# Two cross-attention layers on one core: half products in another order, two of them moved ahead of layer 0's last batch, layer 1's first scores moved ahead of the last query product, and a last pass in two halves

## The chip, the cores and the metric

The kernel runs on one core of a Trainium2 chip, in float32. The metric is the device time of one execution in microseconds (us); lower is better. A difference is judged between medians of runs made on the same chip.

## The reference, cut to what matters

There are 8 batches. `x` is (8, 100, 1024), the context `c` is (8, 1444, 512). Layer 0 is ordinary cross attention with an output projection, layer 1 takes its softmax over the 100 queries (axis 1) instead of over the keys and ends in a layer norm:

```python
# layer 0, per batch
Q = x @ Wq + bq;  K = c @ Wk + bk;  V = c @ Wv + bv
w = softmax(Q @ K.T / 32, axis=keys)
x = x + (w @ V) @ Wo + bo
# layer 1, per batch
q = x @ Wq + bq;  k = c @ Wk + bk;  v = c @ Wv + bv
w = softmax(q @ k.T / 32, axis=queries)
x = w @ v + x
out = (x - mean) * rsqrt(var + 1e-6) * gamma + beta
```

## The kernel before, in words

**Products of weights first.** The kernel never forms K or V. It multiplies Wq by Wk transposed once for each layer (`weight_products` "qk0", "qk1") and Wv by Wo ("vo0"). For a batch it then needs three things: `gT`, the queries times the first product (`queries`, 4 batches of 100 queries side by side in a half, so 400 columns); the scores, `gT` times the context's features (`scores`); and `A`, the weights times the context's rows (`weighted_rows`). `A` is projected at the end: for layer 0 by `project0` for all 8 batches at once, for layer 1 by `project1_halves` (batches 0 to 4), `project1` (5 and 6) and `project_last` (7).

**Seven products for eight.** `queries`, `project0` (twice, j = 0 and 1, tiles `o0_0` and `o0_1`) and `project1_halves` are block products of a 2 by 2 matrix of weight blocks A11, A12, A21, A22 and a 2 by 2 matrix of data blocks B11, B21, B12, B22. `seven_products` computes them with seven half products instead of eight, on sums of blocks: S[0] to S[3] of the A's (`left_sums`), T_[0] to T_[3] of the B's (`right_sums`), made by VectorE (DVE) in between. A half product accumulates in a pair of PSUM banks: X, Z and Y from a pool of 6 banks, W from a pool of 2. X is used three times in a row without being cleared: A11·B11, then S[1]·T_[1] on top, then S[2]·T_[2] on top. After each of these its content is copied or added into one of the four results. `put` is the first write of a result (ScalarE, ACT, in `queries`; an addition into `xT` on DVE elsewhere), `add` a later addition on DVE.

**Order.** TensorE's (PE's) order is the order of the program text (`tc.manual_schedule(engines={PE})`); the other engines' instructions are put in order by the tile framework's scheduler, each engine then running its own list strictly in order, with semaphores in between. In the program text: weight products, `queries(0)`, scores of batches 0 and 1, then for each batch b `alternated`: 48 steps, each one piece of A of batch b and one piece of the scores of batch b+2 (44 pieces). For b = 5 in each layer it takes two pieces of scores a step (`doubled`). Then `project0`, `queries(1)`, the key biases of layer 1 (`key_biases`, tile `c1`), scores of batches 0 and 1 of layer 1, and the 8 steps of `alternated` for layer 1 with the projections.

**Softmax and transposes.** Scores lie with the queries on the partitions and the weights must lie with the keys on them. Layer 0 does its softmax first (`softmax0`) and then transposes: on DVE in 16 instructions (`transposed`, L562), except that for batches 0 and 7 the first 4 of 12 key blocks are transposed on PE (`first_transposed`, tile `pT`, L578) and DVE does the other 8. Layer 1 transposes first and then takes the softmax by groups of 4 key blocks (`softmax_rows`); batch 0's 12 blocks are all transposed on PE, in three groups between the scores of batch 1 (`first_rows`).

**GpSimd (POOL)** makes layer 1's weight sums (`weight_sums`, tiles `part` and `wsum`), the block sums of the last weight (`wv_s`, eight additions) in the buffer that `qk1` leaves when the last query product has read it, and a part of each batch's end. **The end** of a batch is `normalise`: `rstd` on POOL, then for batch 7 three quarters of the row on DVE and one quarter on ACT and POOL, each followed by its store (SP's and ACT's queue).

Of the kernel before, what the change touches and what calls it, by code (L numbers as in the profile page):

```python
# [25 lines left out]
AF = mybir.ActivationFunctionType  # L26
ALU = mybir.AluOpType
# [26 lines left out]
def two_layer_cross_attention(ctx: ExitStack, tc: tile.TileContext, a: dict, out: bass.AP):  # L54
# [11 lines left out]
    def bank(name):  # L66
        return psum.tile([P, 512], F32, tag="ps", name=name)

    def bank2(name):
        return psum2.tile([P, 512], F32, tag="ps2", name=name)  # L70
# [48 lines left out]
    for t in prob:  # L119
        nc.gpsimd.memset(t[T // QD * QD :, :], 0.0)  # L120
        nc.gpsimd.memset(t[:, S:], 0.0)

# [39 lines left out]

    def seven_products(name, A, Bs, S, T_, nb, width, put, add, left=None, right=None):

        left, right = left or (lambda n: None), right or (lambda n: None)
        A11, A12, A21, A22 = A
        B11, B21, B12, B22 = Bs  # L170
        X, Z, Y = ([bank(f"{name}_{n}{j}") for j in range(2)] for n in "xzy")
        W = [bank2(f"{name}_w{j}") for j in range(2)]
        half_product(X, A11, B11, True, nb, width)
        put(0, 0, X)
        left(0)
        right(0)
        half_product(Z, A12, B21, True, nb, width)
        left(1)
        right(1)
        add(0, 0, Z)  # L180
        half_product(Y, S[0], T_[0], True, nb, width)
        put(1, 1, Y)
        left(2)
        right(2)
        half_product(X, S[1], T_[1], False, nb, width)
        put(0, 1, X)
        left(3)
        right(3)
        half_product(X, S[2], T_[2], False, nb, width)
        add(1, 1, X)  # L190
        put(1, 0, X)
        half_product(W, A22, T_[3], True, nb, width)
        add(1, 0, W)
        half_product(Y, S[3], B22, False, nb, width)
        add(0, 1, Y)


    def weight_products(name, left, right, l_width, r_width, scaled):
# [175 lines left out]
    def queries(layer, w, u):  # L374

        H = EC // 2

        def half(g):
            return xT[:, :, g * GT : (g + 1) * GT]

        cols = [slice(j * 256, j * 256 + 256) for j in range(2)]
        A11, A12, A21, A22 = ([w[:, k * H + i, c] for i in range(H)] for c in cols for k in range(2))
        Bs = [[half(g)[:, k * H + i, :] for i in range(H)] for g in range(2) for k in range(2)]
        S1, S2 = (chunks(row(f"g{layer}_s{n}").rearrange("p (c l) -> p c l", c=H), H) for n in (1, 2))
        T1, T2 = (chunks(wide(f"g{layer}_t{n}"), H) for n in (1, 2))
        T3 = chunks(work.tile([P, LC, GT], F32, tag="gT", name=f"g{layer}_t3", bufs=3), H)
        dst = [work.tile([P, LC, GT], F32, tag="gT", name=f"g{layer}T_{g}", bufs=3) for g in range(2)]
        A, S, T_ = (A11, A12, A21, A22), (S1, S2, A21, A12), (T1, T2, T3, T2)

        def put(r, g, banks):  # L390
            for j in range(2):
                c = 2 * r + j
                nc.scalar.activation(dst[g][:, c, :], banks[j][:, :GT], AF.Identity, bias=u[:, c : c + 1])  # L393

        def add(r, g, banks):
            for j in range(2):
                to = dst[g][:, 2 * r + j, :]
                nc.vector.tensor_tensor(to, to, banks[j][:, :GT], ALU.add)

        seven_products(  # L400
            f"g{layer}",
            A,
            Bs,
            S,
            T_,
            2,
            GT,
            put,
            add,
            lambda n: left_sums(A, S, (n,)),  # L410
            lambda n: right_sums(Bs, T_, (n,)),
        )
        return dst


    wqk0, (acc_c, acc_u) = weight_products(
# [11 lines left out]
    block_sums("u0", acc_u, sums_u)  # L428
    sums_c = quarter_sums("c0")
    block_sums("wqbk0", acc_c, sums_c[:, :EC, :])  # L430
    gT = [queries(0, wqk0, totals("u0", sums_u, LC)), None]
    block_sums("bvo", acc_o, sums_c[:, EC:, :])
    got = totals("wqbk0", sums_c, 2 * EC)
    wqbk0 = got[:, :EC]
# [104 lines left out]
    def softmax0(s, parts):  # L539

        b, p = s["b"], s["p"]
        maxima = small.tile([T, len(parts)], F32, tag="maxima", name=f"maxima_{b}")
        for n, part in enumerate(parts):
            nc.vector.tensor_reduce(maxima[:, n : n + 1], p[:, part], AX.X, ALU.max)  # L544
        negmax = small.tile([T, 1], F32, tag="negmax", name=f"negmax_{b}")
        nc.vector.tensor_reduce(negmax, maxima, AX.X, ALU.max, negate=True)
        total = small.tile([T, 1], F32, tag="total", name=f"total_{b}")
        nc.scalar.activation(p, p, AF.Exp, bias=negmax, accum_out=total)
        rtotal = small.tile([T, 1], F32, tag="rtotal", name=f"rtotal_{b}")
        nc.vector.reciprocal(rtotal, total)  # L550
        nc.scalar.activation(p, p, AF.Copy, scale=rtotal)
        transposed(s, PT if b in (0, B - 1) else 0)

    def transposed(s, m0):

# [45 lines left out]
    def project0(AS, A0):  # L601

        Bs = [[A0[g][:, 2 * k + i, :] for i in range(2)] for g in range(2) for k in range(2)]
        t12, t4 = (work.tile([P, LC, GT], F32, tag="gT", name=f"o0_t{n}", bufs=3) for n in (12, 4))
        T_ = ([t12[:, i, :] for i in range(2)], [t12[:, 2 + i, :] for i in range(2)], Bs[2], chunks(t4, 2))
        for j, (A, S) in enumerate(AS):

            def add(r, g, banks):
                e = 4 * j + 2 * r
                add_to_queries([e, e + 1], g * GT, GT, banks)  # L610

            right = None if j else (lambda n: right_sums(Bs, T_, (n,)))
            seven_products(f"o0_{j}", A, Bs, S, T_, 2, GT, add, add, right=right)


    def softmax1(s, parts):

        if s["b"]:
            transposed(s, 0)
            for m in range(0, MC, GM):  # L620
                softmax_rows(s, m)
            weight_sums(s)

    def softmax_rows(s, m0):
        b, w, r = s["b"], s["w"], shown(m0)
# [48 lines left out]
    def project1_halves(A, S, At):  # L674

        n = G1 * T // 2
        Bs = [[At[:, 2 * k + i, g * n : (g + 1) * n] for i in range(2)] for g in range(2) for k in range(2)]
        t1 = work.tile([P, LC, GT], F32, tag="gT", name="o1_t1", bufs=3).rearrange("p c t -> p (c t)")
        T_ = ([t1[:, i * n : (i + 1) * n] for i in range(2)], Bs[0], Bs[2], Bs[1])

        def add(r, g, banks):
            add_to_queries([4 * r + i for i in range(4)], g * n, n, banks)

        seven_products("o1", A, Bs, S, T_, 4, n, add, add, right=lambda k: right_sums(Bs, T_, (k,)))

    def project1(b0, n, A, between):

# [39 lines left out]
    def normalise(s):  # L727
# [7 lines left out]
        if b < B - 1:  # L735
# [1 line left out]
            nc.gpsimd.tensor_tensor(z, z, beta[:T], ALU.add)  # L737
            nc.gpsimd.dma_start(out=out[b], in_=z)
            return
        w, rest = slice(0, 3 * E // 4), slice(3 * E // 4, E)  # L740
        nc.scalar.activation(z[:, rest], z[:, rest], AF.Copy, scale=rstd)
        nc.gpsimd.tensor_tensor(z[:, rest], z[:, rest], beta[:T, rest], ALU.add)
        nc.vector.scalar_tensor_tensor(z[:, w], z[:, w], rstd, beta[:T, w], ALU.mult, ALU.add)
        nc.sync.dma_start(out=out[b][:, w], in_=z[:, w])
        nc.scalar.dma_start(out=out[b][:, rest], in_=z[:, rest])

    def finish(s):

# [18 lines left out]
    batches = [{"b": b} for b in range(B)]  # L767
    A0 = [wide(f"A0T_{g}") for g in range(2)]

    def run(*parts):  # L770

        parts = list(parts)
        while parts:
            parts = [g for g in parts if next(g, parts) is not parts]

    def loaded(*loads):

        got = [[] for _ in loads]
# [2 lines left out]
                to.append(next(load))  # L781
        return got

    def first_scores(layer, softmax, between):

        for b in range(2):
            steps = scores(batches[b], layer, *loaded(load_features(b)), softmax, alone=True)
            for n in range(LC * NB):
                next(steps)
                if b == 1 and n in between:  # L790
                    between[n]()

    def alternated(b, layer, softmax, dst, doubled=False):

# [11 lines left out]
            yield  # L806

    key_bias = [c0, None]
    first_scores(0, softmax0, {LC * NB - 3: lambda: first_transposed(batches[0], 0)})
    for b in range(B):  # L810
        steps = alternated(b, 0, softmax0, A0[b // G][:, :, b % G * T : (b % G + 1) * T], b + 3 == B)
        for n, _ in enumerate(steps):
            if (b, n) == (B - 2, MC * LC - PT - 1):
                first_transposed(batches[B - 1], 0)
        if b == 1:
            AS = value_sums(wvo)
    project0(AS, A0)

    gT[1] = queries(1, wqk1, u1)
    kb1 = [key_bias_sums(f"kb1_{g}", g * GT, (g + 1) * GT, wqbk1) for g in range(B // G)]  # L820
    key_bias[1] = key_biases("c1", kb1, bqbk1)
    vectors = [unit(f"vectors_{j}") for j in range(2)]
    gamma, beta = (t[:, :E] for t in vectors)
# [5 lines left out]
    wv1 = weights.tile([P, LC, E], F32, tag="w", name="wv1")  # L829
    nc.gpsimd.dma_start(out=wv1, in_=a["L1_xattn_Wv"].rearrange("(c p) e -> p c e", p=P))  # L830

    def first_rows(m0):
        first_transposed(batches[0], m0)
        softmax_rows(batches[0], m0)
        if m0 == MC - GM:
            weight_sums(batches[0])

    first_scores(1, softmax1, {5 + m0 // 2: lambda m0=m0: first_rows(m0) for m0 in range(0, MC, GM)})
    A1 = {}

    finished = {(B - 2, 0): 0, (B - 2, 14): 1, (B - 2, 28): 2, (B - 1, 6): G1, (B - 1, 22): G1 + 1}
# [49 lines left out]
```

## Time and profile before

| | us |
|---|---|
| median of 3 runs | 648.43 (647.94 to 648.45) |
| profiled execution, its own time | 647.25 |
| its span, first to last instruction | 645.5 |
| PE busy in the span | 634.1 |
| DVE busy | 438.8 |
| ACT busy | 134.6 |
| POOL busy | 102.4 |
| granted PE clock | 0.997 |

The profiled execution took 1.75 us more than its span. Times in the text are from the span's start. A line of the timeline gives start, length, engine, source line, operation, output<-input, shapes, count, and in square brackets how long the engine had been idle and what released it. PE is the matmul row, PEld the weight loads, which run ahead of it. The trace has two records for each float32 matmul, so a half product of 8 matmuls is "x16". The chain of waits shows, in order of time, the work that ended last at each moment.

### The profile page before, as it was taken

Reading aid. Unit: us, or ns where it says so; the run is one execution under the profiler, and the core shown is the slowest. Engines: PE = TensorE matmul, PEld = TensorE weight load, DVE = VectorE, ACT = ScalarE, POOL = GpSimd, SP = SyncE. Lnnn points to the kernel's source line nnn. Section 1 sums busy time; section 2 is a strip of 40 time slices with the busy share of each in tenths; the row PEclk is TensorE's granted clock in tenths of the full one; section 3 lists DMA queues with packets and bytes.
Section 4 is the critical chain, followed back from the end, with each engine's and each line's share of the span. In section 5 each row is a group of like instructions: output and inputs, shape, how many; then the busy total and the mean of one; then the engine's idle time right before and its main releaser. Section 6 shows DMA issues by size and latency. Waiting matters only on the chain.

```text
span 645.5 us, 9860 instructions
## 1 busy us (share of the span) xinstructions
PE 634.1 (98%) x3936; PEld 519.3 (80%) x3936; DVE 438.8 (68%) x831; ACT 134.6 (21%) x342; POOL 102.4 (16%) x122
## 2 busy tenths in 40 slices
PE   9999999999999999999999999999999999999994
PEld 8886445568885999999998555557999999989992
DVE  5999959569624775566753887214767655896994
ACT  1010010100204223322320000205433244330221
POOL 5000000019100000000010000052210222211773
PEclk9999999999999999999999999999999999999998
DMA  8937027000099789988997003037889889930122
GB/s 296 384 103 301 0 91 295 0 1 0 2 322 348 270 307 318 315 301 318 316 331 261 1 1 131 0 104 275 298 285 329 315 295 324 318 124 1 52 79 74
DMA packets 47961, 127.28 MB, mean 197 GB/s; under 512 B 3944, under 2 KB 6604, under 8 KB 47916
## 3 DMA queue, kind: packets, MB, share of 16 engines
q1 hardware_dynamic: 45454, 119.73, 53.5%
q0 software_dynamic: 2064, 6.56, 3.1%
q8 instruction: 31, 0.51, 0.3%
q10 hardware_dynamic: 398, 0.36, 0.2%
q14 instruction: 14, 0.11, 0.1%
HBM read 123.36 MB, written 3.28 MB: 196 GB/s over the span
## 4 chain that ended last, share of the span: by engine, by line
PE 84%; issue 5%; POOL 5%; DVE 3%; ACT 2%; POOLq 0%; ACTq 0%; DVEq 0%
PE s L515 23%; PE A L486 20%; PE qk_x L135 7%; PE g_x L135 5%; PE qk_y L135 4%; PE g_y L135 3%; PE vo_x L135 3%; DVE w L562 3%; PE o_x L135 3%; POOL z L737 2%; PE qk_w L135 2%; PE qk_z L135 2%; PE vo_y L135 2%; PE o_y L135 2%; PE g_w L135 2%
## 5 line engine op out<-in xcount | busy, mean ns | idle before, releaser
L486 PE MATMUL A<-w,c 120*128 120x100 f32 (+1 forms) x1536 | 242.8, 266 | 0.0
L486 PEld LDWEIGHTS A<-w,c 120*128 120x128 f32 (+1 forms) x1536 | 213.6, 190 | 0.5
L562 DVE STREAM_TRANSPOSE w<-prob 32x384 f32<-32x384 f32 (+1 forms) x240 | 132.4, 552 | 38.1 <-POOL wsum L654 16.6
L515 PE MATMUL s<-cT,g1T 128*100 128x131 f32 (+2 forms) x592 | 119.4, 296 | 0.0
L515 PE MATMUL s<-cT,g0T 128*100 128x131 f32 (+2 forms) x592 | 119.0, 296 | 0.0
L515 PEld LDWEIGHTS s<-cT,g0T 128*100 128x100 f32 x592 | 77.6, 167 | 8.3
L515 PEld LDWEIGHTS s<-cT,g1T 128*100 128x100 f32 x592 | 77.5, 167 | 7.7
L527 ACT ACTIVATE prob<-s,c 100x393 f32<-100x393 f32 (+2 forms) x64 | 35.1, 559 | 123.3 <-PE s L515 122.9
L632 ACT ACTIVATE w<-w,negmax 120x100 f32<-120x100 f32 (+1 forms) x96 | 34.8, 364 | 65.5 <-DVE negmax L630 65.5
L442 POOL TENSOR_SCALAR xT<-xT,L_xattn_bo 128x800 f32<-128x800 f32 x8 | 20.7, 2607 | 133.0 <-PE qk_x L135 133.0
L544 DVE TENSOR_REDUCE maxima<-prob 100x1 f32<-100x394 f32 (+3 forms) x32 | 16.3, 528 | 24.1 <-ACT prob L527 23.8
L135 PE MATMUL qk_x<-qk 128*128 128x256 f32 x128 | 29.5, 390 | 0.0
L649 POOL TENSOR_TENSOR part<-w 120x500 f32<-120x500 f32 x8 | 10.0, 1246 | 114.8 <-PE s L515 47.3
L135 PEld LDWEIGHTS qk_x<-qk 128*128 128x128 f32 x128 | 24.7, 197 | 4.0 <-ACT qk L253 0.4
L826 POOL DMA_DIRECT2D vectors<-in_L_xattn_gamma x1 | 0.6, 602 | 161.9 <-DVE rtotal L550 161.9
L630 DVE TENSOR_REDUCE negmax<-w 120x4 f32<-120x400 f32 (+1 forms) x24 | 12.7, 555 | 13.2 <-ACT w L579 13.1
L277 DVE SCALAR_TENSOR_TENSOR qk_L_xattn_bk<-qk,L_xattn_bk,qk_L_xattn_bk 128x1024 f32<-128x1024 f32 x14 | 17.9, 1280 | 3.4 <-DMA qk<-in_L_xattn_WqT 3.3
L632 ACT ACTIVATION_READ_ACCUMULATOR w<-w,negmax 120x1 f32 (+1 forms) x96 | 17.9, 186 | 0.0
L737 POOL TENSOR_TENSOR z<-z,vectors 100x1024 f32<-100x1024 f32 x7 | 16.5, 2356 | 8.3 <-ACT z L736 8.3
L393 ACT ACTIVATE g1T<-g_x,k 128x400 f32<-128x400 f32 x6 | 3.6, 594 | 63.4 <-PE g_x L135 58.1
L585 DVE TENSOR_TENSOR xT<-xT,o_x 128x400 f32<-128x400 f32 (+1 forms) x24 | 13.6, 601 | 4.5 <-PE o_x L135 4.2
L736 ACT ACTIVATE z<-z,rstd 100x1024 f32<-100x1024 f32 x7 | 8.0, 1148 | 41.2 <-POOL rstd L733 41.1
(218 smaller groups left out, 881.3 us busy)
## 6 DMA issues: line engine op xcount, KB each, us to landing
cT<-in_ctxT SPq DMA_DIRECT2D x64, 722.0 KB, 6.6
c<-in_ctx SPq DMA_DIRECT2D x48, 768.0 KB, 6.2
c<-in_ctx SPq DMA_DIRECT2D x16, 512.0 KB, 6.6
vo<-in_L_xattn_Wo SPq DMA_DIRECT2D x8, 512.0 KB, 6.8
qk<-in_L_xattn_WqT SPq DMA_DIRECT2D x8, 512.0 KB
qk<-in_L_xattn_WqT SPq DMA_DIRECT2D x15, 256.0 KB, 5.4
qk<-in_L_xattn_WkT SPq DMA_DIRECT2D x15, 256.0 KB, 6.2
c<-in_ctx SPq DMA_DIRECT2D x16, 224.0 KB, 5.9
```

The source lines that it names most:

```text
L135: nc.tensor.matmul(banks[n // per][:, n % per * width : (n % per + 1) * width], lhs[i][:, n * P : (n + 1) * P], rhs[i], start=(fresh and i ...
L277: nc.vector.scalar_tensor_tensor(acc, src, cols[v][:, h : h + 1], acc, ALU.mult, ALU.add)
L442: nc.gpsimd.tensor_scalar(xT[:, e, :], xT[:, e, :], out_bias[:, e : e + 1], None, ALU.add)
L486: nc.tensor.matmul(ps[:, k * T : (k + 1) * T], c[m // CQ][:r, m % CQ, k * P : (k + 1) * P], w[:r, m, :], start=(m == 0 and k == 0), stop=( ...
L515: nc.tensor.matmul(banks[n // per][:T, cuts[n] - o : cuts[n + 1] - o], q[:, k, t0 : t0 + T], cT[k][:, cuts[n] : cuts[n + 1]], start=(k == ...
L527: nc.scalar.activation(p[:, part], ps[:T, : part.stop - part.start], AF.Identity, bias=key_bias[layer][:T, b : b + 1], scale=SCALE,)
L544: nc.vector.tensor_reduce(maxima[:, n : n + 1], p[:, part], AX.X, ALU.max)
L562: nc.vector.transpose(blocks(w, r, m0 * T + q * QD, T, MC - m0), blocks(p, q, m0 * MR + r * QD, MR, MC - m0),)
L585: nc.vector.tensor_tensor(to, to, ps[:, : n * width].rearrange("p (n t) -> p n t", n=n), ALU.add)
L630: nc.vector.tensor_reduce(negmax[:r], w[:r, grp, :], AX.X, ALU.max, negate=True)
L632: nc.scalar.activation(w[:r, m0 + m, :], w[:r, m0 + m, :], AF.Exp, bias=negmax[:r, m : m + 1], accum_out=total[:r, m : m + 1])
L737: nc.gpsimd.tensor_tensor(z, z, beta[:T], ALU.add)
```

## The change

Six things, with their place in the code.

1. `seven_products` is a generator with a `yield` after each product. W (A22·T_[3]) moves from sixth to fifth place, between the second and the third use of X, and `right(3)` moves ahead of the second one. In `queries` T_[3] is written into T1's buffer instead of T2's.
2. `project0` yields its two generators. Before layer 0's batch 7 the first two products of `o0_0` (A11·B11 and A12·B21, which need batches 0 to 3 alone) are run; after it the first product of `o0_1`, then the rest.
3. Layer 0's b = 5 is no longer doubled, and batch 7's weights are all transposed on DVE (16 instructions over 12 blocks instead of 8; the 4 PE transposes and their ACT copy go).
4. In layer 1 six of the seven query products are issued, then the key biases' sum, then batch 0's scores, then the seventh product (S[3]·B22 into Y), then batch 1's scores.
5. In layer 1 batch 0's weights are transposed on DVE (16 instructions) and go through the same `softmax1` as the others; the 12 PE transposes and their three ACT copies go.
6. `normalise` for batch 7: two halves on DVE, the first stored by SP's queue, the second by ACT's; the ACT and POOL quarter goes.

On the engines: PE has the same matmuls less 16 transposes; SP's list is the same but for one store's size; POOL's list loses one instruction.

```diff
     def seven_products(...):
...
+        X = pair("x")
+        product(X, A11, B11, True)
         put(0, 0, X)
+        yield
+        Z = pair("z")
+        product(Z, A12, B21, True)
+        yield
         left(0)
         right(0)
-        half_product(Z, A12, B21, True, nb, width)
         left(1)
         right(1)
         add(0, 0, Z)
-        half_product(Y, S[0], T_[0], True, nb, width)
+        Y = pair("y")
+        product(Y, S[0], T_[0], True)
         put(1, 1, Y)
+        yield
+        right(3)
+        product(X, S[1], T_[1], False)
+        put(0, 1, X)
+        yield
         left(2)
         right(2)
-        half_product(X, S[1], T_[1], False, nb, width)
-        put(0, 1, X)
+        W = pair("w", bank2)
+        product(W, A22, T_[3], True)
+        yield
         left(3)
-        right(3)
-        half_product(X, S[2], T_[2], False, nb, width)
+        product(X, S[2], T_[2], False)
         add(1, 1, X)
         put(1, 0, X)
-        half_product(W, A22, T_[3], True, nb, width)
         add(1, 0, W)
-        half_product(Y, S[3], B22, False, nb, width)
+        yield
+        product(Y, S[3], B22, False)
         add(0, 1, Y)
+        yield
...
-        A, S, T_ = (A11, A12, A21, A22), (S1, S2, A21, A12), (T1, T2, T3, T2)
+        A, S, T_ = (A11, A12, A21, A22), (S1, S2, A21, A12), (T1, T2, T3, T1)
...
-        transposed(s, PT if b in (0, B - 1) else 0)
+        transposed(s, 0 if b else PT)
...
     for b in range(B):
-        steps = alternated(b, 0, softmax0, ..., b + 3 == B)
-        for n, _ in enumerate(steps):
-            if (b, n) == (B - 2, MC * LC - PT - 1):
-                first_transposed(batches[B - 1], 0)
+        if b == B - 1:
+            o0 = list(project0(AS, A0))
+            next(o0[0])
+            next(o0[0])
+        run(alternated(b, 0, softmax0, ...))
...
-    project0(AS, A0)
-    gT[1] = queries(1, wqk1, u1)
+    next(o0[1])
+    for steps in o0:
+        run(steps)
+    gT[1], steps = queries(1, wqk1, u1)
+    for n in range(6):
+        next(steps)
...
-    first_scores(1, softmax1, {5 + m0 // 2: lambda m0=m0: first_rows(m0) for m0 in range(0, MC, GM)})
+    run(first_scores(0, 1, softmax1))
+    run(steps)
+    run(first_scores(1, 1, softmax1))
...
-        w, rest = slice(0, 3 * E // 4), slice(3 * E // 4, E)
-        nc.scalar.activation(z[:, rest], z[:, rest], AF.Copy, scale=rstd)
-        nc.gpsimd.tensor_tensor(z[:, rest], z[:, rest], beta[:T, rest], ALU.add)
-        nc.vector.scalar_tensor_tensor(z[:, w], z[:, w], rstd, beta[:T, w], ALU.mult, ALU.add)
-        nc.sync.dma_start(out=out[b][:, w], in_=z[:, w])
-        nc.scalar.dma_start(out=out[b][:, rest], in_=z[:, rest])
+        for half, queue in ((slice(0, E // 2), nc.sync), (slice(E // 2, E), nc.scalar)):
+            nc.vector.scalar_tensor_tensor(z[:, half], z[:, half], rstd, beta[:T, half], ALU.mult, ALU.add)
+            queue.dma_start(out=out[b][:, half], in_=z[:, half])
```

## The prediction

> **What bounds the kernel now.** First the table of busy time, then the chain of waits, then the timeline where the chain shows a gap.
>
> ```profile
> PE 634.1 (98%) x3936; PEld 519.3 (80%) x3936; DVE 438.8 (68%) x831; ACT 134.6 (21%) x342; POOL 102.4 (16%) x122
> ```
>
> PE is busy 634.1 of 645.5 us, so time can only come from three places: PE work that goes, holes that the busy figure hides (a matmul's end is modelled), and the tail after PE's last product. The chain around the half products shows hidden holes:
>
> ```profile
> 404.21 5.37 PE g_x L135 x16
> 409.58 0.01 issue
> 409.59 5.64 PE g_x L135 x16
> 415.24 5.37 PE g_w L135 x16
> ```
>
> Equal products take 5.37 us, the third use of X 5.64. The weight loads, ACT and, for layer 1's projection, PE say why:
>
> ```profile
> 409.59 0.30 PEld L135 LDWEIGHTS g_x<-g_t,qk 128*128 128x128 f32 x2 [0.65 <-ACT g1T L393]
> 415.28 1.27 ACT L393 ACTIVATE g1T<-g_x,k 128x400 f32<-128x400 f32 x2 [5.06 <-DVE g1T L398]
> 575.56 3.54 PE L135 MATMUL o_x<-A1T,wv_s 128*128 128x250 f32 x16
> 580.35 3.64 PE L135 MATMUL o_x<-A1T,wv_s 128*128 128x250 f32 x16 [1.26 <-DVE xT L585]
> ```
>
> PE waits for ACT to copy X out before it adds the next product onto X; in `project1_halves` it waits for DVE. The second line also shows that ACT's copy of a bank starts only when DVE's addition from that bank is done. PE's other avoidable work is its transposes and the doubled batch:
>
> ```profile
> 308.25 0.45 PE s L515 x4
> ...
> 322.36 15.61 PE A L486 x140
> 337.97 0.34 PE pT L578 x4
> ...
> 439.56 0.35 PE pT L578 x4
> ...
> 441.13 0.34 PE pT L578 x4
> ...
> 442.69 0.35 PE pT L578 x4
> ```
>
> [...] a piece of A alone (128 weight columns, 100 moving) takes 15.61/70 = 0.223 us, and alternated with a score piece (100 weight columns, 131 moving) the pair takes 0.4275 (446.52 to 446.95). [...] batch 4's L734 took 3.34 us at 609.32 beside POOL's addition that ended at 611.58, against 1.28 elsewhere, but 16 DVE transposes kept 0.591 each beside POOL's sums at 448.
>
> **The change part by part.**
>
> *W between X and X.* The hole goes where a product of W's length hides the copy: 5.64 − 5.37 = 0.27 in each `queries` (124.64 and 409.59), 5.63 − 2·2.69 = 0.25 in each half of `project0` (358.01, 377.08), and in `project1_halves` 580.35 − 575.56 − 3.38 = 1.41 plus 0.10 of a slow restart. Sum 2.55 us. What W now needs earlier is T_[3]. In `queries` its first write waits until Y has read T1: done about 0.6 us after Y's end, W starts 5.37 after it. In `project1_halves` its second block comes after the Y additions, at 579.71 before; W would start at 578.94 and reach that block at 580.63, so 0.9 us is left. In layer 0's `queries` the next weight product's first DVE sums take T1's buffer and so wait for W (130.0 instead of 119.3), with X's additions of this product queued behind them; they are for a product that starts at 155, and X's banks are next needed at 141 to 148. I take nothing.
>
> *PE transposes.* Batch 7: 0.35. Layer 1's batch 0: 1.04. Sum 1.39, and four ACT copies off the path. DVE gets 16 transposes of 12 blocks instead of 8 (9.46 against 7.32 us), and 16 new ones (9.46).
>
> *Batch 5 not doubled.* Before, 22 steps of one A and two score pieces took 14.11 (308.25 to 322.36) and the 22 A pieces that follow 22·0.223 = 4.91: 19.02. Taken per step, 0.651·22 + 4.91 = 19.23. Now 44·0.4275 = 18.81. Gain 0.2 to 0.4; I take 0.4.
>
> *Does batch 7 still come in time?* Its scores now end with b = 5's 44th step, at 308.03 + 18.81 = 326.84, and A of batch 5 at 327.7. Batch 6, never doubled, shows the chain that follows: A of batch 4 ended at 308.03 and DVE's last of 16 transposes at 312.15 + 9.46 = 321.61, 13.6 later. So batch 7's weights are there at 341.3. PE reaches A of batch 7 at 327.7 + 48·0.223 = 338.4 without the two products of `o0_0`: 2.9 us too early. They add 2·2.69 = 5.38, to 343.8: covered by 2.5 us. DVE then adds them to `xT` beside A of batch 7. They are the same products, so PE gains and loses nothing by the move. After batch 7, Y of `o0_0` needs T_[0], two sums behind the copy of A: copy and sums took from 349.97 to 351.64 before, 1.7 us; the first product of `o0_1` covers 2.69.
>
> *Layer 1's start.* With E the end of the sixth query product, batch 0's scores need banks. The key biases' sum and the first score piece take free ones; the second and third take X's, held until ACT's copy, which waits for DVE's addition. Read from 415.07 to 416.55, ACT is done at E + 0.8 and E + 1.5; the pieces are due at E + 0.75 and E + 1.36. Lost: 0.1 to 0.35, I take 0.2. The fourth waits for DVE's reading of the key-bias bank, at about E + 1.6, and is due later. Call S the scores' end (16 pieces of 0.611). The seventh product (5.37) and batch 1's scores (9.77) follow: A of batch 0 starts at S + 15.1. By the rows of batch 1 before, DVE starts to transpose at S + 0.65, ends at S + 10.1, and the first four blocks' softmax is done 3.4 later; one addition of the seventh product, 0.5, is in DVE's list between. Ready at S + 14.0, 1.1 us early. But POOL's eight sums now fall here:
>
> ```profile
> 426.07 2.49 POOL L146 TENSOR_TENSOR wv_s<-wv 128x512 f32<-128x512 f32 x2 [39.61 <-PE g_y L135]
> ```
>
> They start when the seventh product ends, S + 5.4, and last 9.8 us, to S + 15.2. DVE's first multiplication (L636, two SBUF inputs) can wait for one of them, 1.25: lost 0 to 0.3, I take 0.1. POOL's weight sums of batch 0 start at S + 16.5; their transpose on PE comes a batch later.
>
> *The end.* DVE's 768 columns end at 640.51 and ACT's store is issued at 641.12, behind POOL's quarter, which waited for DVE. Two halves of 0.69 from 639.49 let the last store be issued at about 640.9: 0.2 gained, against 200 KB instead of 100 KB on that queue. No row shows how long a lone store of each size takes; POOL's 400 KB stores landed in 3.2 us. Between −0.3 and +0.3; I take +0.1. DVE, ACT and POOL before it follow PE's products and move with them.
>
> **Sum.** 2.55 + 1.39 + 0.4 − 0.2 − 0.1 + 0.1 = 4.1 us of 647.25, giving 643.1 for such an execution. That one ran 1.2 under the median of 648.43; against the median, **644.3**. Everything gained lies on PE before its last product, so nothing is taken off twice.
>
> **The rivals.**
>
> *Covers partly fail.* DVE runs in order, and each start (A of batch 7, `project0`'s Y, A of layer 1's batch 0) has a margin of only 1 to 2.5 us. If one or two are late by 1 to 2 us more than the rows say, the gain is 1.5 to 3.2: about 646. For it: the margins. Against: the chains were read off equal batches, and DVE is 33.35 of 38 us busy in 350 to 388, where the change takes four additions away.
>
> *DVE behind POOL at layer 1's start: slower.* If POOL's eight sums keep DVE out for their whole length, DVE's chain of batch 0 stretches by up to 9.9 us. 1.1 is margin, so PE stands up to 8.8 us at A of batch 0: 648.43 − 4.1 + 8.8 = 653.1. It decides from a delay of 1.1 + 4.1 = 5.2 us. For it: the 3.34 us above. Against: transposes have run beside POOL undisturbed[...].
>
> *Holes move.* If W's product only moves the wait (T_[3] late in each of the five places by as much as the hole was), 2.55 goes and the rest, 1.6 less small losses, stays: 646.9. Against: DVE had T_[3]'s sums done in 2 to 3 us in all three kinds of place. That PE's transposes do not go, or that the order is not what the text says, is excluded by the instruction lists.
>
> **How the numbers follow.** Forecast (gain 3.2 to 4.9, its own range 643.5 to 645.2) 0.65; covers partly fail 0.14; holes move 0.06; little net, within 0.2% (1.3 us, about what a measurement of this kernel can tell from no change), 0.06; slower 0.09. Faster: 0.65 + 0.14 + 0.06 = 0.85; same 0.06; slower 0.09. The range reaches from the best bounds (no losses, +0.3 at the end: 643.2) to the partly failed covers, 646.9.
>
> **What would show it.** Right: all products of a `queries` at 5.37 and none of `project1_halves` with an idle PE before it; PE with 16 transposes (32 records) less; A of batch 7 starting at once behind `o0_0`'s second product, with DVE's transposes ended some 2.5 us before; layer 1's second score piece 0.1 to 0.35 late. Wrong: PE waiting for DVE transposes or L636 ahead of an A, for `g_t` or `A1T` sums ahead of a W, or more than 1 us ahead of layer 1's scores; DVE multiplications of 1 us and more beside `wv_s`.

## The result, and the profile after

The changed kernel takes 642.29 us, median of 4 runs (642.10 to 643.39), against 648.18 us for the kernel before beside it (4 runs, 647.19 to 648.45): ratio 0.9915, 95% interval 0.9898 to 0.9932. Run again later (e12 below), it took 642.62 us against 647.45: ratio 0.9926 (0.9914 to 0.9939), 4.8 us. The direction was right; 642.3 lies 0.9 us below the range on record (643.2 to 646.9). The two profiled executions differ by 647.25 − 642.46 = 4.8 us, in their spans (first to last instruction) by 645.5 − 640.7, again 4.8.

The busy times of the page after:

```profile
PE 631.4 (99%) x3920; PEld 518.4 (81%) x3920; DVE 450.0 (70%) x848; ACT 132.2 (21%) x337; POOL 101.7 (16%) x121
```

PE has 16 matmuls fewer and 2.7 us less busy time; DVE has 17 instructions and 11 us more. So 4.8 us cannot all be PE work that went. The chain of waits of the kernel after, first in layer 0's `queries`, then around its last batch, then at layer 1's start (start, length, what):

```profile
124.97 5.37 PE g_w L141 x16
130.35 5.37 PE g_x L141 x16
```

```profile
326.84 11.59 PE A L513 x104
338.43 2.71 PE o_x L141 x8
341.14 2.69 PE o_z L141 x8
343.83 10.70 PE A L513 x96
```

```profile
413.66 5.37 PE g_x L141 x16
419.03 0.14 PE c L348 x2
419.17 9.98 PE s L542 x32
429.15 5.37 PE g_y L141 x16
434.52 9.73 PE s L542 x32
444.25 0.20 PE A L513 x2
```

The third use of X takes 5.37 us, no longer 5.64. A of batch 7 follows the second product of `o0_0` with nothing in between, and A of layer 1's batch 0 follows batch 1's scores. No engine but PE stands in these three chains. The timeline of layer 0's end and layer 1's start shows how near the others were:

```profile
331.83 9.46 DVE L589 STREAM_TRANSPOSE w<-prob 32x384 f32<-32x384 f32 x16 [1.56 <-ACT prob L578]
...
419.07 1.27 ACT L418 ACTIVATE g1T<-g_x,k 128x400 f32<-128x400 f32 x2 [10.15 <-DVE g1T L423]
419.71 0.25 PEld L542 LDWEIGHTS s<-cT,g1T 128*100 128x100 f32 x2 [0.48 <-ACT g1T L418]
420.39 3.60 PEld L542 LDWEIGHTS s<-cT,g1T 128*100 128x100 f32 x13 [0.42 <-ACT g1T L418]
...
441.98 2.83 POOL L152 TENSOR_TENSOR wv_s<-wv,wv_s 128x512 f32<-128x512 f32 x2
442.49 1.18 DVE L662 TENSOR_TENSOR w<-w,rtotal 120x400 f32<-120x400 f32 x1
443.80 1.44 DVE L662 TENSOR_TENSOR w<-w,rtotal 120x400 f32<-120x400 f32 x1
445.36 0.57 DVE L662 TENSOR_TENSOR w<-w,rtotal 124x400 f32<-124x400 f32 x1
```

Batch 7's transposes end at 331.83 + 9.46 = 341.29, 2.5 us ahead of PE. The second and third score pieces of layer 1 wait for ACT's copies of X's banks (the two weight-load lines released by ACT): batch 0's scores take 9.98 us against batch 1's 9.73, so 0.25 us is lost. DVE's multiplications beside POOL's sums take 1.18 and 1.44 us, alone 0.57; yet the chain shows no wait of PE for them. In `project1_halves` (timeline) the products follow each other at 3.375 us (579.88 − 576.50 = 3.38) with no idle PE between them:

```profile
576.50 3.54 PE L141 MATMUL o_w<-A1T,wv 128*128 128x250 f32 x16
...
579.88 3.54 PE L141 MATMUL o_x<-A1T,wv_s 128*128 128x250 f32 x16
```

The gain can be read along the way, always the time before less the time after. At A of layer 1's batch 0: 446.52 − 444.25 = 2.27. At the last product of `project_last`: 629.44 − 625.48 = 3.96. At `rstd`'s arrival at DVE for batch 7: 639.49 − 635.54 = 3.95. At the end of the span: 4.8. So the last 0.85 us comes from what lies behind `rstd`: the end. Its lines are, before,

```profile
639.49 1.02 DVE L743 SCALAR_TENSOR_TENSOR z<-z,rstd,vectors 100x768 f32<-100x768 f32 x1 [0.46 <-POOL rstd L733]
640.54 0.31 SPq L744 DMA_DIRECT2D out<-z  x1
641.12 0.57 ACTq L745 DMA_DIRECT2D out<-z  x1
```

and after

```profile
635.54 1.41 DVE L767 SCALAR_TENSOR_TENSOR z<-z,rstd,vectors 100x512 f32<-100x512 f32 x2 [0.46 <-POOL rstd L759]
636.32 0.31 SPq L768 DMA_DIRECT2D out<-z  x1
636.99 0.57 ACTq L768 DMA_DIRECT2D out<-z  x1
```

The SPq and ACTq lines are where the two engines issue their stores.

### The profile page after: what moved, and what is told of

Its sections match the earlier page's. It is cut to its first block, busy times and chain, and to the rows that moved or that the text cites. A ratio compares the mean times of both kernels' runs of the same rounds, so it can differ in the third digit from the quotient of the medians.

```text
span 640.7 us, 9823 instructions
## 1 busy us (share of the span) xinstructions
PE 631.4 (99%) x3920; PEld 518.4 (81%) x3920; DVE 450.0 (70%) x848; ACT 132.2 (21%) x337; POOL 101.7 (16%) x121
## 4 chain that ended last, share of the span: by engine, by line
PE 84%; issue 5%; POOL 5%; DVE 4%; ACT 2%; POOLq 0%; DVEq 0%; ACTq 0%
PE s L542 23%; PE A L513 20%; PE qk_x L141 7%; PE g_x L141 5%; PE qk_y L141 4%; PE g_y L141 3%; PE vo_x L141 3%; DVE w L589 3%; PE o_x L141 3%; POOL z L763 2%; PE qk_w L141 2%; PE vo_y L141 2%; PE qk_z L141 2%; PE g_w L141 2%; PE g_z L141 2%
## 5 line engine op out<-in xcount | busy, mean ns | idle before, releaser
L513 PE MATMUL A<-w,c 120*128 120x100 f32 (+1 forms) x1536 | 245.9, 265 | 0.0
L589 DVE STREAM_TRANSPOSE w<-prob 32x384 f32<-32x384 f32 (+1 forms) x256 | 143.7, 561 | 46.4 <-ACT prob L554 15.8
L542 PE MATMUL s<-cT,g0T 128*100 128x131 f32 (+2 forms) x592 | 122.7, 296 | 0.0
L662 DVE TENSOR_TENSOR w<-w,rtotal 120x400 f32<-120x400 f32 (+1 forms) x24 | 15.2, 633 | 0.5
```

The lines of the kernel that those rows point to most:

```text
L513: nc.tensor.matmul(ps[:, k * T : (k + 1) * T], c[m // CQ][:r, m % CQ, k * P : (k + 1) * P], w[:r, m, :], start=(m == 0 and k == 0), stop=( ...
L542: nc.tensor.matmul(banks[n // per][:T, cuts[n] - o : cuts[n + 1] - o], q[:, k, t0 : t0 + T], cT[k][:, cuts[n] : cuts[n + 1]], start=(k == ...
L589: nc.vector.transpose(blocks(w, r, m0 * T + q * QD, T, MC - m0), blocks(p, q, m0 * MR + r * QD, MR, MC - m0),)
L662: nc.vector.tensor_tensor(w[:r, grp, :], w[:r, grp, :], rtotal[:r].unsqueeze(2).to_broadcast([r, GM, T]), ALU.mult)
```

## The experiments

All compare with the kernel before on the same chip: 647.46 us (41 runs) for e0, e1, e5 and e7; 647.36 (17 runs) for e2, e3, e4 and e8; 647.45 (14 runs) for e9 to e12. Ratios carry their 95% interval.

### The end: e0, e1, e5, e7, e11

**e0**, the kernel before, with no edit: what a difference of nothing looks like.

> The kernel before, once more, for a second profile. Theory A (the gain was 1.8 us larger than forecast because the first profiled execution was a short one, 1.2 us under its median, and I took that difference over to the changed kernel): the span of this execution is nearer 646.5 than 645.5, and the two profiles differ in a stage where PE waits for data or in the last stores, not in the products. Theory B (the whole excess lies in the changed end): the span is 645.5 within 0.3 again.

647.74 us, ratio 1.0005 (0.9997 to 1.0013); its profiled span was 646.0, not 645.5. A single profiled execution of one and the same kernel moves by half a microsecond, so the 4.8 us between the two profiles is not better than that.

**e1**, before with the new end alone:

```diff
-        w, rest = slice(0, 3 * E // 4), slice(3 * E // 4, E)
...
+        for half, queue in ((slice(0, E // 2), nc.sync), (slice(E // 2, E), nc.scalar)):
+            nc.vector.scalar_tensor_tensor(z[:, half], ...)
+            queue.dma_start(out=out[b][:, half], in_=z[:, half])
```

> The kernel before with the new end of the last batch alone (two halves on DVE). My prediction's step: last store issued about 0.2 us earlier, gain 0.1 us (ratio 0.9998). Theory B (the end saves what the two profiles show, 0.84 us from rstd to the end of the span): gain 0.7 to 0.9 us (ratio 0.9987). Theory A: the end's length differs from run to run by as much as 0.7 us, and the gain is 0.2 to 0.4.

646.69 us, ratio 0.9986 (0.9980 to 0.9993): 0.9 us by the ratio, between 0.45 and 1.3. The end alone is worth more than the prediction's upper bound of 0.3; theory B, which had read 0.7 to 0.9 from the two profiles, holds.

**e7**, before with three quarters and one quarter, both on DVE. It takes ACT's and POOL's part away but keeps stores of 300 and 100 KB:

```diff
-        w, rest = slice(0, 3 * E // 4), slice(3 * E // 4, E)
...
+        for part, queue in ((slice(0, 3 * E // 4), nc.sync), (slice(3 * E // 4, E), nc.scalar)):
+            nc.vector.scalar_tensor_tensor(z[:, part], ...)
+            queue.dma_start(out=out[b][:, part], in_=z[:, part])
```

> The kernel before with the old cut of the last batch (768 and 256 columns, stores of 300 and 100 KB), but both parts on DVE, so that neither ACT nor POOL is in the end. If the sizes of the stores set the 0.67 us between last store and end of span: the end stays as long as before after the last store (4.4 us), gain 0.2. If POOL's part at the end did: 3.7 us after the last store, gain 0.8 as with the halves.

647.55 us, ratio 0.9998 (0.9989 to 1.0006): nothing gained, although POOL's wait for DVE is gone and the last store is issued 641.03 − 639.58 = 1.45 us after `rstd`, as early as in the changed kernel (636.99 − 635.54 = 1.45; before, 1.63). What is left to matter is the size of the stores, and with it the moment of the first, which DVE's first part sets.

**e5**, the changed kernel with the old end:

```diff
-        for half, queue in ((slice(0, E // 2), nc.sync), (slice(E // 2, E), nc.scalar)):
...
+        w, rest = slice(0, 3 * E // 4), slice(3 * E // 4, E)
...
```

> The changed kernel with the old end of the last batch. Prediction's step: 0.1 us slower than the changed kernel, so 642.4 against 648.2 (ratio 0.9911). Theory B: 0.8 slower, 643.1 (ratio 0.9921).

643.09 us, ratio 0.9933 (0.9921 to 0.9946). Against e12's 0.9926 the intervals overlap, so the times alone don't show the end here; the traces are sharper (table below).

**e11**, the changed kernel with a half and two quarters:

```diff
-        for half, queue in ((slice(0, E // 2), nc.sync), (slice(E // 2, E), nc.scalar)):
+        parts = (slice(0, E // 2), nc.sync), (slice(E // 2, 3 * E // 4), nc.scalar), (slice(3 * E // 4, E), nc.sync)
+        for half, queue in parts:
```

> The changed kernel with the last pass in three parts, 512 columns to SP, 256 to ACT's queue, 256 to SP's. The last store is issued at the same time or 0.1 later than in the changed kernel and carries 100 KB instead of 200 KB; the 200 KB store is issued at the same time. Theory A (what ends the span is the time from the last issue to the landing, shorter for a smaller store): 0.2 to 0.4 us less than the changed kernel. Theory B (it is the fixed part of a store, and rows of 1 KB are moved no faster in sum): within 0.2 us of it, as with three quarters and one quarter before.

642.40 us, ratio 0.9921 (0.9908 to 0.9933), not to be told from e12 by the times, and both traces take 5.1 us from `rstd` to the end: a smaller last store brings nothing there while the first stays at 200 KB.

The traces of these kernels, put side by side:

| kernel | stores, KB | from `rstd` at DVE to the end of the span | from SP's first store issue to the end |
|---|---|---|---|
| before | 300, 100 | 645.5 − 639.49 = 6.0 | 645.5 − 640.54 = 4.95 |
| e0 | 300, 100 | 6.0 | 4.95 |
| e7 | 300, 100 | 5.9 | 4.9 |
| e5 | 300, 100 | 6.0 | 4.95 |
| e1 | 200, 200 | 5.1 | 4.35 |
| after | 200, 200 | 640.7 − 635.54 = 5.2 | 640.7 − 636.32 = 4.4 |
| e12 | 200, 200 | 5.1 | 4.3 |
| e11 | 200, 100, 100 | 5.1 | 4.35 |

The size of SP's first store sorts them without exception: 4.9 to 5.0 us for 300 KB, 4.3 to 4.4 us for 200 KB; which engine made the last part does not. Each store has 100 packets of one row (3072, 1024 or 2048 bytes before and after, with 10 packets of 4 bytes beside them), so its size and its packets' length change together.

The DMA view of narrow windows (queue, packets, MB, share of 16 engines' time; q1 is SP's queue, q10 ACT's) tells why. Before, from 641 to 642.8 us and from 642.8 to 643.4:

```profile
q1 hardware_dynamic: 71, 0.22, 52.2%
```

```profile
q1 hardware_dynamic: 35, 0.09, 36.8%
q10 hardware_dynamic: 46, 0.05, 21.3%
```

After, from 636.8 to 637.9 and from 637.8 to 638.2:

```profile
q1 hardware_dynamic: 55, 0.11, 44.8%
```

```profile
q1 hardware_dynamic: 46, 0.09, 57.7%
q10 hardware_dynamic: 2, 0.00, 2.6%
```

ACT's store was issued at 641.12 before, and none of its packets moves until 642.88, 1.8 us later: until then only packets of SP's store move, and about two thirds of it are through. After, ACT's store is issued at 636.99 and moves from 638.14, 1.15 us later, when nearly three quarters of SP's are through. From ACT's issue to the end: 645.5 − 641.12 = 4.4 before, 640.7 − 636.99 = 3.7 after.

The packets' own times in the profiles before and after show that the start of the second store went with the first store rather than with its own issue. Its first packet comes 1.57 us after the first store's first packet with 300 KB ahead (641.31 and 642.88, before) and 1.04 with 200 KB ahead (637.10 and 638.14, after), although ACT's issue comes 0.58 us behind SP's before and 0.67 after. In e7 (300 KB ahead) and e11 (200 KB ahead) it comes only 0.40 behind: e7's second store has no packet from 642 to 642.6 and two between 642.6 and 643, 2.0 to 2.4 us after SP's issue (before, 2.34); e11's has none from 637 to 638 and five by 638.2, so it begins 1.75 to 1.95 us after SP's issue (after, 1.82) and at least 1.35 after its own (after, 1.15). From its first packet to its last the second store then takes about 1.2 us both times (1.16 before, 1.18 after), with 100 KB and with 200. That doesn't mean that its own size is free: before, 99 KB of the first store still moved beside it, after, 54 KB. That the second store starts late behind the first is read off these traces; what in the DMA engines makes it so was not tried.

### The order, and the moves without it: e2, e8

**e2**, before with W's product between the second and third use of X (item 1 of the change), nothing else; **e8**, the changed kernel with the old order. The core of e8's diff (e2 has these moves the other way round; both also change T_[3]'s buffer in `queries`):

```diff
-        right(3)
+        left(2)
+        right(2)
         product(X, S[1], T_[1], False)
         put(0, 1, X)
         yield
-        left(2)
-        right(2)
-        W = pair("w", bank2)
-        product(W, A22, T_[3], True)
-        yield
         left(3)
+        right(3)
         product(X, S[2], T_[2], False)
         add(1, 1, X)
         put(1, 0, X)
+        yield
+        W = pair("w", bank2)
+        product(W, A22, T_[3], True)
...
```

> The kernel before with the new order of the seven products alone (W between the second and third use of X, T_[3] in T1's buffer). Prediction's step: the five holes go, 0.27 + 0.27 + 0.25 + 0.25 + 1.51, gain 2.55 us (ratio 0.9961). Rival (holes move): T_[3] is late by as much, gain under 0.5 us (ratio 0.999 or more).

644.67 us, ratio 0.9960 (0.9946 to 0.9973): 2.6 to 2.7 us (1.7 to 3.5 by the interval), against the prediction's 2.55. In its trace the third use of X in layer 0's `queries` takes 5.37 and the products of `project1_halves` stand 3.37 to 3.38 apart: the holes went and did not move.

> The changed kernel with the old order of the seven products (the other parts kept). Prediction's step: 2.55 us back, less the 0.2 us of the bank wait at layer 1's first scores, which the old order doesn't have: 2.3 us slower than the changed kernel, 644.6 against 648.2 (ratio 0.9945). Rival: 642.3 to 642.8 (ratio 0.991).

645.32 us, ratio 0.9967 (0.9955 to 0.9980): 2.0 to 2.1 us against before (1.3 to 2.9 by the interval). Its third use of X takes 5.64 again (124.45 to 130.10). 2.7 for the order and 2.0 for the rest make 4.7, and the whole, e12, is 4.8: within these intervals the parts add up. Less the end's 0.8 to 0.9, the moves and the transposes are worth 1.1 to 1.2, give or take about 0.9.

### The covers: e3, e4, e9, e10

A cover is work put where PE would otherwise wait for another engine.

**e3**, the changed kernel without the two products ahead of layer 0's last batch:

```diff
         if b == B - 1:
             o0 = list(project0(AS, A0))
-            next(o0[0])
-            next(o0[0])
         run(alternated(b, 0, softmax0, ...))
...
+    next(o0[0])
+    next(o0[0])
     next(o0[1])
```

> The changed kernel with the first two products of o0_0 back behind batch 7 (batch 7 not doubled, all its transposes on DVE). If the two products are the cover that I worked out: PE reaches A of batch 7 at 338.4 and waits 2.9 us for the last DVE transpose at 341.3, 645.2 (ratio 0.9954). Rival (they cover nothing that costs): 642.3.

656.81 us, ratio 1.0139 (1.0125 to 1.0153): not the few microseconds of a wait, but 9 us slower than before. The wait is what the prediction worked out for it, 2.9 us: the chain calls it "issue", but DVE's last transpose of batch 7 ends at 341.67 and A begins at 341.77. The chain shows what else happened:

```profile
338.83 2.94 issue
341.77 20.77 PE A L513 x96
362.55 3.82 PE o_x L141 x8
```

A of batch 7 took 20.77 us instead of 10.70, the next product 3.82 instead of 2.71. PE waits for nothing in that stretch; the windows view (columns: length, then PE, weight loads, DVE, ACT, POOL busy, granted clock, DMA share, GB/s) names it:

```profile
338.00:341.00 3.00, 0.82 (x8) 0.65 (x6) 2.88 (x6) 0.00 (x0) 0.00 (x0) 0.96 1.02 404
341.00:364.00 23.00, 22.23 (x99) 21.60 (x100) 2.60 (x6) 0.00 (x0) 0.00 (x0) 0.50 0.38 126
364.00:367.00 3.00, 3.00 (x9) 1.65 (x9) 1.94 (x5) 0.00 (x0) 0.00 (x0) 0.89 0.56 216
```

The granted clock fell to a half, 0.50, from 341 − 2·0.04·3 = 340.8 to 364 + 2·0.11·3 = 364.7: 23.9 us. The lost time is 2.94 + (20.77 − 10.70 = 10.07) + (3.82 − 2.71 = 1.11) = 14.1 of the 14.5 us between this span and the changed kernel's. All four executions took 655.25 to 656.98 us, so the loss was there each time.

**e4**, the changed kernel with the seventh query product ahead of layer 1's first scores:

```diff
-    run(first_scores(0, 1, softmax1))
     run(steps)
+    run(first_scores(0, 1, softmax1))
     run(first_scores(1, 1, softmax1))
```

> The changed kernel with the seventh query product of layer 1 back ahead of batch 0's scores (batch 0 still all on DVE). If it is the cover that I worked out: PE reaches A of batch 0 9.8 us after batch 0's scores, its weights are ready after about 13.5, so PE waits 3.7 us and saves the 0.2 us bank wait: 645.8 (ratio 0.9963). Rival (batch 1's scores cover enough): 642.3 or a little less.

648.69 us, ratio 1.0013 (1.0005 to 1.0021): a little slower than before, 5.6 us more than e12 by the ratios. Eight of its 13 executions took 648.6 to 649.1 us and five 647.3 to 647.8; what parts them can't be told from the one profile, which is of the first group. Its timeline and its windows:

```profile
448.55 0.43 PE L513 MATMUL A<-w,c 120*128 120x100 f32 x2 [3.79 <-issue]
```

```profile
449.00:450.00 1.00, 1.00 (x9) 1.00 (x8) 0.57 (x1) 1.00 (x7) 0.00 (x0) 0.73 0.10 34
450.00:452.00 2.00, 2.00 (x12) 2.00 (x11) 1.19 (x3) 1.53 (x5) 0.85 (x1) 0.50 0.00 0
452.00:453.00 1.00, 1.00 (x7) 1.00 (x7) 0.94 (x3) 0.00 (x0) 1.00 (x3) 0.57 0.00 0
```

A wait of 3.79 us (for batch 0's weights: DVE's first multiplication ends at 448.44), then a half clock for 0.54 + 2 + 0.86 = 3.4 us, in which pieces of A and of scores take 0.38 and 0.44 us instead of 0.20 and 0.23: half of it is lost, 1.7. Together 5.5.

**e9** separates the wait from the clock: e3 with PE kept busy where it had waited, on matmuls that nobody reads.

```diff
             o0 = list(project0(AS, A0))
+            fill = bank("fill")
+            for _ in range(12):
+                nc.tensor.matmul(fill[:, :P], ones, ones, start=True, stop=True)
```

> No products of o0_0 ahead of layer 0's last batch, but 12 matmuls of the array of ones (128 columns, into a bank that nothing reads) stand where TensorE waited 2.94 us: 12 pairs of records at about 0.225 us, 2.7 us. They add work and take nothing from what is waited for; A of batch 7 starts at the same moment as without them. Theory A (the wait itself cost 2.9 us, the other 11.5 us came from TensorE's clock, which fell to half after the wait for 23.9 us): the clock stays at 1.0, A of batch 7 takes 10.7 us again, and the time is that of the changed kernel plus 2.9: about 645.2, ratio to before 0.9965. Theory B (the loss came from work that became late behind the last batch, whatever the clock): near 656, ratio 1.014.

645.44 us, ratio 0.9971 (0.9962 to 0.9981), 11 us less than e3 by added useless work. PE in its timeline:

```profile
337.62 2.87 PE L833 MATMUL fill<-ones 128*128 128x128 f32 x24
340.74 10.93 PE L513 MATMUL A<-w,c 120*128 120x100 f32 x96 [0.26 <-PE fill L833]
```

The clock stays at 1.00 in the windows that follow, one of which is

```profile
345.00:350.00 5.00, 5.00 (x47) 5.00 (x47) 0.00 (x0) 0.00 (x0) 0.00 (x0) 1.00 0.83 284
```

and A takes 10.93 us. A of batch 7 still starts 2.9 us late behind the useless work, and this costs e9 2.8 us against e12; the other 11 us of e3 went with the clock's fall.

**e10**, one product ahead instead of two:

```diff
             o0 = list(project0(AS, A0))
             next(o0[0])
-            next(o0[0])
         run(alternated(b, 0, softmax0, ...))
...
+    next(o0[0])
     next(o0[1])
```

> The changed kernel with one product of o0_0 ahead of layer 0's last batch, the second behind it. TensorE comes to A of batch 7 2.7 us after the end of A of batch 6, at about 341.1 of the profile, and the weights are there at 341.3: a wait of 0.2 to 0.4 us. Theory A (only a wait of some us makes the clock fall): 642.3 + 0.3 = 642.6, ratio 0.992. Theory B (any wait at this place costs the clock, or the second product is needed as cover): 645 to 654.

642.94 us, ratio 0.9931 (0.9918 to 0.9943), the same as e12 within the intervals. PE waits 0.24 us, A takes 10.93 as in e9, and the clock's mean over the span is 0.998 (e3: 0.979):

```profile
341.01 10.93 PE L513 MATMUL A<-w,c 120*128 120x100 f32 x96 [0.24 <-PE o_x L141]
```

**e12**, the changed kernel again, with no edit:

> The changed kernel as it is, to set its gain by more runs. By the sum of the parts alone, measured on their own (order 2.65, end 0.9, the two moves together about 1.4, 2.1 less the end's 0.9 plus what rounding leaves), 4.8 to 5.1 us, ratio 0.9921 to 0.9926. If the first comparison's 5.9 us is right, 0.991.

642.62 us (641.96 to 643.36, 5 runs), ratio 0.9926. None of the variants beats it beyond the intervals.

## Why the prediction was wrong by a little, point by point

**W between X and X: right.** Forecast 2.55, measured 2.6 to 2.7 alone (e2). The interval, 1.7 to 3.5, is wide, but in the trace of the changed kernel the products of `queries`, `project0` and `project1_halves` follow each other at 5.37, 2.69 and 3.38 us without a hole: T_[3] was in time at all five places, so the rival "holes move" is out.

**Transposes, batch 5, layer 1's start: right.** Forecast 1.39 + 0.4 − 0.2 − 0.1 = 1.5. In the traces: 2.27 at A of layer 1's batch 0, plus 0.33 by which this execution began later (its first products stand that much later already at 54.99, `vo_x`, against 54.66), less W's parts before it, 0.27 + 0.27 + 0.50: 1.56. The bank wait was 0.25 (forecast 0.2). Two multiplications did run longer beside POOL's sums as feared, by 0.6 and 0.9 us, but this cost PE nothing: the first group's ended at 442.49 + 1.18 = 443.67, and A was due at 444.25. e8, by times instead of traces, gives 1.1 to 1.2, with an uncertainty of about 0.9 that takes in both.

**The covers: right in time, wrong in price.** Batch 7's weights were ready at 341.29 (forecast 341.3), A of batch 7 began at 343.83 (343.8); without the cover PE waited 2.94 (2.9). But the rival "covers partly fail" priced a late start at its own length. Measured, a wait of 2.94 us cost 14 and one of 3.79 cost 5.5, because TensorE's clock fell to 0.50, for 23.9 and 3.4 us; only the wait of 0.24 cost about itself. So pricing a wait at its length was wrong at 3 to 4 us: covers failing by that much gave 656.8 and 648.7. What the rival's own 1 to 2 us would cost, no run shows. The covers did not fail, so this did not move the result. The rival "DVE behind POOL: slower" named the right engines and instructions, but the delay was 1.5 us, and it decides from 5.2: each multiplication lost less than one of POOL's additions lasts (2.49/2 = 1.25 us), and only the last two of POOL's eight were still to run then (from 441.98). (One count of the prediction was off: the 16 transposes leave 16 records on PE, not 32; their time, 1.39 us, was read from the rows and holds.)

**The end: the term that failed.** Forecast +0.1 between −0.3 and +0.3; measured 0.85 in the traces and 0.9 (0.45 to 1.3) alone in e1. The mistake was to give each store a time of its own, counted from its own issue: 0.2 gained by the earlier last issue, less a loss because ACT's queue carries 200 KB instead of 100 KB. The earlier issue came as forecast (1.45 us after `rstd` instead of 1.63), but e7 has the same and gained nothing. What the traces show in its place is that the first store leads. It is issued 640.54 − 639.49 = 1.05 us after `rstd` before and 636.32 − 635.54 = 0.78 after, since DVE's first part is shorter: 0.27. The second store's packets begin 1.57 us after the first's before and 1.04 after: 0.53. These two make 0.80 of the 0.85; what follows took nearly the same time in both. No run changes one of the two without the other. The loss feared from the larger second store did not show in the end; less of the first one was left to move beside it (54 KB against 99).

**From the profile to the median: the second error.** The sum gave 643.1 for an execution like the profiled one, and I added 1.2 because the profiled one lay that far under the median of 648.43. That median came of three runs; three later comparisons gave 647.46, 647.36 and 647.45 in 72 runs, so 647.25 was an ordinary execution and the offset mostly chance. Without it and with the end at 0.85, the same sum gives 647.25 − 4.9 = 642.4. The two errors, 0.75 at the end and 1.2 here, are the 2.0 us between 644.3 and the measured 642.3. The first comparison's 5.9 us carries the same chance: its four runs of the kernel before are these three and one more, and e12 gives 4.8. Whether that chip was slower for the kernel before can't be told from four runs; for the changed kernel it was not (642.29 there, 642.62 in e12).

**The range's lower end** was not what its own terms give. No losses and +0.3 at the end make 2.55 + 1.39 + 0.4 + 0.3 = 4.64, so 648.43 − 4.64 = 643.8, not 643.2.

## What to carry to other kernels

Price the last stores together, not each by itself: of two on two queues here, the second started when the first was two thirds to three quarters through, and 200 KB twice beat 300 KB followed by 100 KB by 0.85 us. When work is moved so that the busiest engine just doesn't wait, ask what a failed cover costs including the clock: if a wait of some microseconds on TensorE can't be avoided, useless matmuls in it can be cheaper than the silence, here by 11 us for a wait of 2.9. And take the offset between a profiled execution and a median of three runs as noise until more runs say otherwise.

## What the runs showed of the hardware that was not expected

A wait was followed by a fall of TensorE's granted clock from 1.00 to 0.50 in e3 and e4 (from 341 to 364 in e3's windows and from 450 to 452 in e4's it is 0.50), and not in e9, whose windows from 337 to 353 all have 1.00. Behind the 2.94 us of e3 stood 23.9 us at 0.50, behind the 3.79 us of e4 3.4 us, and the 0.24 us of e10 left A at 10.93 us. In e3 the fall came within the wait, 1.9 us after it began (340.8 against 338.83). In e4 it came 4.7 us after the wait began (449.5 against 448.55 − 3.79 = 444.76), 0.9 us after the work had resumed. Of these two the longer wait had the later fall and the shorter half clock; what sets either was not tried.

Why the clock came back after 3.4 us in e4 and after 23.9 in e3 was not tried either. What the traces show: in e4 pieces of A and of scores alternated, in e3 pieces of A alone ran for 20.77 us, and the clock rose 2.1 us after the first product with 400 columns had begun (364.7 against 362.55). Before the wait, A alone had run for 11.6 us at 1.00 (from 327.23), so the same pieces ran at the full clock before the wait and at half of it after. No run here separates the kind of work from other causes.
